# Layer 1 of a two-layer graph kernel: the mask added on four 64x64 tiles of TensorE, and six of 32 steps in which VectorE multiplies two heads

## The chip, the cores and the metric

The kernel runs on one core of a Trainium2 chip. The metric is the device time of one execution in microseconds (us); three runs are shown for the kernel before. A separate, profiled execution gives the trace from which all durations are taken.

## The reference

The input is `x` (4096 x 512) and a sparse matrix `adj` (4096 x 4096), nonzero on about 1.6% of its places and on the diagonal. Layer 0 is attention with an additive bias of 2 x `adj`; layer 1 is graph attention with eight heads of 64 features. The change touches layer 1 only:

```python
nX = (x @ W).reshape(n, NHEAD, OUT_DIM).transpose(1, 0, 2)
# nX is normalized over its 64 features
at1 = jnp.einsum('kno,ok->kn', nX, a1)[:, :, None]
at2 = jnp.einsum('kno,ok->kn', nX, a2)[:, :, None]
kg = jax.nn.leaky_relu(at1 + at2.transpose(0, 2, 1), negative_slope=LK_ALPHA)
kg = kg * graph[None, :, :]
mg = jnp.where(mask[None, :, :], kg, NEG_FILL)
attention = jax.nn.softmax(mg, axis=-1)
y = attention @ nX + nX
return jax.nn.elu(y)
```

So for each head and each pair of nodes there is a logit, the leaky ReLU of a sum of two numbers, multiplied by the edge's weight `graph`, masked where there is no edge, and put through an exponential before it weighs the features.

## The kernel before, in words

Layer 1 works on the transposed scores: sources lie on the 128 partitions, 512 target nodes on the free axis. A **step** is one block of 128 sources for 512 targets and four heads. There are 8 chunks of targets, 2 halves of the heads and 32 source blocks, so 512 steps. The 32 steps of one chunk and one half of the heads are called a **group** here (16 groups, 0 to 15). All engines follow an order that is written out by hand (`seq` keeps every instruction in program order on its engine). The loop over `n` runs, for each step: `values(n - 4)`, `exponent(n - 3)`, `leaky(n)`, `weigh(n)`, `z_sums(n + 1)`, `relu(n + 1)`.

- `z_sums` (TensorE, L955): for each of the four heads a matmul of six rows, `z2` against `z1` (L964), puts the sum of the two attention numbers into PSUM. The heads use different groups of 32 rows of the array. Then a matmul with the 128x128 identity (L969) adds the mask `nb`, which is a huge negative number where there is no edge. There are three PSUM tiles `d` of two banks each; a step needs two of them, one for heads 0 and 1 and one for heads 2 and 3.
- `relu` (ScalarE, L976) starts the leaky ReLU of heads 0 and 1 and writes the tile `t`, of which there are six.
- `leaky` (VectorE): two scalar_tensor_tensor instructions (L986) make the leaky ReLU of heads 3 and 2, a tensor_tensor (L991) multiplies by the edge weights `g`, and another (L992) completes heads 0 and 1.
- `weigh` (GpSimd, called POOL in profiles, L999) multiplies the heads that VectorE didn't by `g`.
- `exponent` (ScalarE, L1002) takes the exponential of all four heads in place.
- `values` (TensorE, L1015) multiplies `t` by the features `nX` in fp32, two heads side by side on 64 columns each, and accumulates over the group's 32 steps.

How the edge-weight multiply is shared is set by the set `light`: in an ordinary step VectorE multiplies one head and GpSimd three; in a step in `light` each multiplies two.

```python
light = {n + d for n in range(NB + 3, n_steps, NB) for d in (9, 10)}
```

That is steps 12 and 13 of every group but group 0 (30 steps), when GpSimd also has the ELU of the group before.

`finish` closes a group, spread over the first 14 steps of the next: ScalarE copies the sums out of PSUM (L1031), TensorE turns them to rows (L1037), VectorE divides (L1046, L1048) and adds the node's own features `own` into a tile `y` (L1049), ScalarE and GpSimd make the ELU (L1059 to L1077), and the rows are stored (L1081). `load_rows` (L947) loads `xi` and `own` for it from step 12 of a group on, on the queue of SP.

`load_adj` (L905) loads, on SP's queue and once per four steps, what the next four steps need: `z2`, the masks `nb` and the weights `g`. Each has two buffers. Group 0 also loads the features, and prepares the last 512 rows of layer 0's output (`make_ready`), some of it on GpSimd; the `own` products that `make_ready` spreads out reach into groups 1 to 4 (L360, L361).

Of the kernel before, what the change touches and what calls it, by code (L numbers as in the profile page):

```python
# [10 lines left out]
F32 = mybir.dt.float32  # L11
BF16 = mybir.dt.bfloat16
# [6 lines left out]
P = 128  # L19
N = 4096  # L20
D = 512
NH = 8
HD = 64
NB = N // P
SB = 4
# [10 lines left out]
GC = 512  # L36
# [42 lines left out]
def fast_path(  # L79
# [18 lines left out]
    nc = tc.nc  # L98
    seq = tc.keep_in_program_order
# [13 lines left out]
    const = ctx.enter_context(tc.tile_pool(name="const", bufs=1))  # L113
# [4 lines left out]
    ident_b = const.tile([P, P], BF16, name="ident_b")  # L118
# [24 lines left out]
    nT_d = dram.tile([NB, P, N], BF16, name="nT_d")  # L143
# [30 lines left out]
        return mv  # L174


    aa = [const.tile([P, NH, HD], F32, name=f"a{e}_sb") for e in (1, 2)]
    aln_sb = const.tile([P, HD], F32, name="aln_sb")
    bln2_sb = const.tile([P, HD], F32, name="bln2_sb")
    at_b = const.tile([P, 2, NH], F32, name="at_b")  # L180
# [279 lines left out]


    with tc.tile_pool(name="early", bufs=2) as early, tc.tile_pool(name="kv", bufs=1) as kv:
        v = kv.tile([P, NB, D], F32, name="v")
        TILES = [(ic, jt) for ic in range(NI) for jt in range(NB)]
        n_tiles = len(TILES)
# [66 lines left out]
        with tc.tile_pool(name="proj_c", bufs=1) as pc, tc.tile_pool(  # L532
            name="proj", bufs=2
# [125 lines left out]
            for k in range(KC):  # L659
                pa_ps = psum.tile([P, 512], F32, name="pa", tag="mm", bufs=4)  # L660
                for c in range(SB):
                    seq(nc.tensor.matmul(
                        pa_ps, turned["q"][:, c, ts(k, P)], turned["k"][:, c, :],
                        start=c == 0, stop=c == SB - 1,
# [6 lines left out]
            for sb in range(1, NS):  # L671
# [4 lines left out]
                if sb == 1:  # L676
                    seq(nc.sync.dma_start(
                        out=w1_sb.rearrange("p k h e -> p k (h e)"),
                        in_=w1.rearrange("(k p) o -> p k o", p=P),
# [16 lines left out]
        with tc.tile_pool(name="attn", bufs=2) as work, tc.tile_pool(  # L696
            name="attn_ps", bufs=2, space=PSUM
# [142 lines left out]
            for s in range(0, n_tiles, 2):  # L840
                ic, jt = TILES[s]
# [48 lines left out]
    with tc.tile_pool(name="ga_in", bufs=2) as inputs, tc.tile_pool(  # L890
# [4 lines left out]
        JB = 4  # L895
# [3 lines left out]
        inverses = gat.tile([P, NI, 2, 2, 2, 4], F32, name="inverses")  # L899
        loads, logits, zs, groups = {}, {}, {}, {}  # L900

        light = {n + d for n in range(NB + 3, n_steps, NB) for d in (9, 10)}
        later = {}

        def load_adj(q):  # L905
            ic, _, jt = STEPS[q * JB]
            z2 = inputs.tile([P, JB * P], BF16, name="z2", tag="z2", bufs=2)
            seq(nc.sync.dma_start(
                out=z2, in_=z2_d[:, STEPS[q * JB][1], jt * P : (jt + JB) * P]
            ))  # L910
            ng = inputs.tile([P, JB, GC], BF16, name="nb", tag="nb", bufs=2)
            seq(nc.sync.dma_start(
                out=ng, in_=nT_d[jt : jt + JB, :, ts(ic, GC)].rearrange("t p i -> p t i")
            ))
            g = adjs.tile([P, JB, GC], F32, name="g", tag="g", bufs=2)
            seq(nc.sync.dma_start(
                out=g, in_=gT_d[jt : jt + JB, :, ts(ic, GC)].rearrange("t p i -> p t i")
            ))
            loads[q] = (g, ng, z2)

        def cols(ic, hg):
            rows = slice(ic * GC, (ic + 1) * GC)
# [32 lines left out]
        def z_sums(n):  # L955

            ic, hg, jt = STEPS[n]
            _, ng, z2 = loads[n // JB]
            pair = [None, None]
            for hf in (1, 0):  # L960
                pair[hf] = psum.tile([P, 2, GC], F32, name="d", tag="d", bufs=3)
            for hh in (2, 3, 0, 1):
                rows = slice(32 * hh, 32 * hh + 6)
                seq(nc.tensor.matmul(  # L964
                    pair[hh // 2][:, hh % 2, :], z2[rows, ts(jt % JB, P)],
                    groups[ic, hg]["z1"][rows, :], start=True, stop=False,
                ))
            for hh in (2, 3, 0, 1):
                seq(nc.tensor.matmul(  # L969
                    pair[hh // 2][:, hh % 2, :], ident_b, ng[:, jt % JB, :], start=False, stop=True  # L970
                ))
            zs[n] = pair

        def relu(n):
# [45 lines left out]
        def finish(n, ic, hg):  # L1020

            grp = groups.pop((ic, hg))
            ob = work.tile([P, 2, GC], F32, name="ob", tag="ob", bufs=1)
            y = work.tile([P, 2, SB * 2, HD], F32, name="y", tag="y", bufs=1)

            def room():
                grp["e"] = work.tile([P, 2, SB * 2, HD], F32, name="e", tag="ob", bufs=1)

            def copies():
                for hf in range(2):  # L1030
                    seq(nc.scalar.copy(ob[:, hf, :], grp["acc"][hf]))  # L1031

            def to_rows(hf):
                pt = psum.tile([P, 2, GC], F32, name="pt1", tag="d", bufs=3)
                for b in range(SB):
                    col = (b % 2) * 2 * HB
                    seq(nc.tensor.matmul(  # L1037
                        pt[:, b // 2, col : col + 2 * HB], ob[:, hf, ts(b, P)],
                        back.rearrange("p e c -> p (e c)"), start=True, stop=True,
                    ))  # L1040
                grp["pt"] = pt[:, :, 0 : 4 * HB].rearrange("p k (q c) -> p k q c", c=HB)

            def divide(hf):
                v = grp.pop("pt")
                rinv = inverses[:, ic, hg, hf]
                seq(nc.vector.reciprocal(rinv, v[:, :, :, HD]))  # L1046
                v = v[:, :, :, 0:HD]
                seq(nc.vector.tensor_mul(v, v, rinv.unsqueeze(3).to_broadcast([P, 2, 4, HD])))  # L1048
                seq(nc.vector.tensor_add(  # L1049
                    y[:, hf].rearrange("p (k q) e -> p k q e", k=2), v,  # L1050
                    grp["own"][:, hf].rearrange("p b d -> p (b d)")
                    .rearrange("p (k q e) -> p k q e", k=2, e=HD),
                ))

            def flat(t):
                return t.rearrange("p f q e -> p (f q e)")

            def minus(hf):
                seq(nc.scalar.activation(grp["e"][:, hf], y[:, hf], AF.Relu, scale=-1.0))  # L1059

            def exps(hf):
                e = grp["e"][:, hf]
                seq(nc.scalar.activation(e, e, AF.Exp, scale=-1.0))

            def positive():
                seq(nc.scalar.activation(flat(y), flat(y), AF.Relu))

            def less_one():
                seq(nc.scalar.add(flat(grp["e"]), flat(grp["e"]), -1.0))

            def elu():
                e = flat(grp["e"])
                seq(nc.gpsimd.tensor_add(e, e, flat(y)))  # L1073

            def close():
                e = grp["e"]
                seq(nc.gpsimd.tensor_add(  # L1077
                    flat(e), flat(e), grp["xi"].rearrange("p f b d -> p (f b d)")
                ))
                for f, ap in enumerate(pair_rows(out, ic, hg)):  # L1080
                    nc.sync.dma_start(  # L1081
                        out=ap, in_=e[:, f].rearrange("p (b h) e -> p b (h e)", h=2)
                    )

            for d, place, f in (
                (0, "mid", copies),
                (1, "mid", lambda: to_rows(0)), (1, "end", lambda: divide(0)),
                (2, "mid", lambda: to_rows(1)), (2, "end", lambda: divide(1)),
                (4, "end", room), (4, "end", lambda: minus(0)), (5, "end", lambda: minus(1)),
                (6, "end", lambda: exps(0)), (6, "end", positive), (7, "end", lambda: exps(1)),  # L1090
                (8, "end", less_one),
                (9, "end", elu), (10, "end", close),
            ):
                later.setdefault((n + d, place), []).append(f)
# [34 lines left out]
        for n in range(n_steps + 15):  # L1129

            q = n // JB + 1
            if n == 1:
                store_rows(NI - 1, last_rows)
            if n % JB == (2 if q == NS - 1 else 0) and q < n_steps // JB:
                load_adj(q)
                if q < NS:
                    load_features(q)
            if n < n_steps and STEPS[n][2] == 12:
                load_rows(n)
            if n + 10 < n_steps and STEPS[n + 10][2] == 0:  # L1140
                open_group(n + 10, nc.sync)
            extra(n, "top")
            if 0 <= n - 4 < n_steps:
                values(n - 4)
                if n % JB == 3:
                    loads.pop((n - 4) // JB)
                if STEPS[n - 4][2] == NB - 1:
                    finish(n, *STEPS[n - 4][:2])
            if 0 <= n - 3 < n_steps:
                exponent(n - 3)  # L1150
            extra(n, "mid")
            for f in left.pop(n, []):
                f()
            if n % JB == 2 and n // JB < NS:
                ones_in(n // JB)
            if n < n_steps:
                leaky(n)
                weigh(n)
            if n + 1 < n_steps:
                z_sums(n + 1)  # L1160
                relu(n + 1)
            for f in left_late.pop(n, []):
                f()
            extra(n, "end")
# [425 lines left out]
```

## Time and profile before

| | |
|---|---|
| median of 3 runs | 3963.34 us (3960.78 to 3963.43) |
| the profiled execution | 3960.13 us, its span 3958.2 us |
| TensorE busy | 3786.1 us, 96% of the span |
| VectorE busy | 2889.7 us, 73% |
| GpSimd busy | 2569.7 us, 65% |
| ScalarE busy | 1796.8 us, 45% |
| layer 1 | about 2080 us to the end |
| DMA in layer 1 | about 45% busy, some 145 GB/s |
| L969, masks | 2048 matmuls, 385 ns each, 536.3 us busy |
| L999, GpSimd's multiplies | 512, mean 3410 ns |

A row of the profile's groups gives the line, the engine, the operation, output and inputs, the shapes and the number of instructions; then the busy time in us and the mean duration in ns; then the idle time of the engine just before them and who ended it. A row of a timeline gives the start in us, the duration, the engine and the group, merged when several alike follow each other (x4). The durations of matmuls overlap because they are pipelined; so do those of VectorE's instructions, by about 0.08 us, and the distance from start to start is then the better measure. The profile calls `z2` and `z1` just `z`, `u4` `u`, and so on, since numbers in names are left out.

### The profile page before, as it was taken

The numbers are of one execution on the slowest core, as the hardware profiler recorded it, in microseconds if no ns is written. First come the engines' busy times: TensorE is split into PE (matmuls) and PEld (weight loads), VectorE is DVE, ScalarE is ACT, GpSimd is POOL, SyncE is SP. The second block draws the span as 40 slices with busy tenths as digits, with TensorE's granted clock in tenths as the row PEclk, the third lists the DMA queues.
The fourth block names the chain that finished last, engine by engine and source line by source line (L and its number), as shares of the span: only waits on it lengthen the run. The fifth ranks groups of instructions, "written<-read, shape, count | busy, mean of one in ns | idle before, by whom it ended". The sixth has DMA issues, their size and how long they took to land. (4 is left out here: it accounts for less than half of the span.)

```text
span 3958.2 us, 44075 instructions
## 1 busy us (share of the span) xinstructions
PE 3786.1 (96%) x15370; PEld 1788.6 (45%) x15370; DVE 2889.7 (73%) x4331; ACT 1796.8 (45%) x1581; POOL 2569.7 (65%) x1305
## 2 busy tenths in 40 slices
PE   8989999999999999999998899999999999999997
PEld 4446666666666666666652222222222222222222
DVE  5435556565565656556557899999999999999996
ACT  1000111111111111111115788888888888888886
POOL 3432225243242525234257999999999999999998
PEclk9999999999999999999998999999999999999999
DMA  6466657667675766768557544444444444444442
GB/s 214 169 213 195 198 175 207 199 194 213 182 220 161 223 182 191 215 183 223 164 158 190 149 141 141 145 146 138 140 138 145 140 146 146 146 139 146 129 151 79
DMA packets 554407, 670.37 MB, mean 169 GB/s; under 512 B 79808, under 2 KB 397504, under 8 KB 534720
## 3 DMA queue, kind: packets, MB, share of 16 engines
q1 hardware_dynamic: 552112, 665.70, 56.5%
q8 instruction: 122, 2.00, 0.2%
q10 hardware_dynamic: 2064, 1.77, 0.2%
q14 instruction: 109, 0.89, 0.1%
HBM read 495.12 MB, written 172.23 MB: 169 GB/s over the span
## 5 line engine op out<-in xcount | busy, mean ns | idle before, releaser
L999 POOL TENSOR_TENSOR t<-t,g 128x1536 f32<-128x1536 f32 (+1 forms) x512 | 1722.8, 3410 | 34.3 <-DVE t L992 29.1
L1015 PE MATMUL acc<-t,nX 128*64 128x512 f32 x4096 | 994.5, 606 | 66.8 <-ACT t L1002 54.5
L751 POOL TENSOR_TENSOR total<-total,aT 128x512 f32<-128x512 f32 x248 | 340.3, 1372 | 1061.3 <-ACT aT L746 1051.1
L1002 ACT ACTIVATE t<-t 128x2048 f32<-128x2048 f32 x512 | 975.9, 1906 | 85.8 <-POOL t L999 84.6
L761 PE MATMUL acc<-v,aT 128*128 128x512 f32 x2048 | 961.9, 592 | 0.0
L746 ACT ACTIVATE aT<-aT 128x512 f32<-128x512 f32 x256 | 161.2, 630 | 1322.8 <-DVE aT L741 1314.8
L992 DVE TENSOR_TENSOR t<-t,d 128x1024 f32<-128x1024 f32 x512 | 619.9, 1211 | 12.3 <-ACT t L976 12.3
L976 ACT ACTIVATE t<-d 128x1024 f32<-128x1024 f32 x512 | 524.8, 1025 | 227.7 <-PE d L969 205.0
L969 PE MATMUL d<-nb,ident_b 128*128 128x512 bf16 x2048 | 536.3, 385 | 1.5 <-DMA nb<-nT_d 1.5
L1015 PEld LDWEIGHTS acc<-t,nX 128*64 128x64 f32 x4096 | 250.4, 136 | 595.3 <-issue 340.1
L761 PEld LDWEIGHTS acc<-v,aT 128*128 128x128 f32 x2048 | 389.7, 190 | 272.4 <-issue 244.9
L986 DVE SCALAR_TENSOR_TENSOR d<-u,at2m,d 128x512 f32<-128x512 f32 x542 | 407.0, 751 | 50.1 <-PE d L969 35.2
L741 DVE TENSOR_TENSOR aT<-aT,X 128x256 f32<-128x256 f32 x512 | 214.9, 420 | 280.5 <-PE X L733 277.3
L986 DVE SCALAR_TENSOR_TENSOR t<-u,at2m,d 128x512 f32<-128x512 f32 x482 | 360.0, 747 | 49.2 <-DVE d L986 0.9
L741 DVE TENSOR_TENSOR aT<-aT,Z 128x256 f32<-128x256 f32 x384 | 159.6, 416 | 292.3 <-PE Z L733 287.6
L991 DVE TENSOR_TENSOR t<-d,g 128x512 f32<-128x512 f32 (+1 forms) x512 | 366.0, 715 | 5.1 <-DMA g<-gT_d 1.8
L725 DVE SCALAR_TENSOR_TENSOR gs<-ng,aT 128x512 f32<-128x512 bf16 x256 | 285.8, 1117 | 10.1 <-DMA gT_d<-gs 1.4
L964 PE MATMUL d<-z,z 6*128 6x512 bf16 x2048 | 250.1, 385 | 35.2 <-DVE t L991 15.4
L964 PEld LDWEIGHTS <-z 6*128 6x128 bf16 x2048 | 76.4, 91 | 443.2 <-issue 439.1
L733 PE MATMUL Z<-qt,hS 128*128 128x256 f32 x1024 | 265.7, 382 | 9.0 <-DVE aT L741 8.3
L969 PEld LDWEIGHTS <-ident_b 128*128 128x128 bf16 x2048 | 159.2, 98 | 241.6 <-issue 121.9
L733 PE MATMUL X<-qt,hS 128*128 128x256 f32 x1024 | 263.8, 380 | 0.0
(170 smaller groups left out, 3124.9 us busy)
## 6 DMA issues: line engine op xcount, KB each, us to landing
g<-gT_d SPq DMA_DIRECT2D x128, 1024.0 KB, 5.5
ag<-in_adj_dram SPq DMA_DIRECT2D x256, 256.0 KB, 5.7
hT<-h_d SPq DMA_DIRECT2D x64, 1024.0 KB, 5.9
hS<-s_d SPq DMA_DIRECT2D x64, 1024.0 KB, 8.3
gT_d<-gs SPq DMA_DIRECT2D x256, 256.0 KB, 3.0
nb<-nT_d SPq DMA_DIRECT2D x128, 512.0 KB, 5.1
nT_d<-ng SPq DMA_DIRECT2D x256, 128.0 KB, 3.4
z<-z_d SPq DMA_DIRECT2D x143, 128.0 KB, 4.7
```

What stands on the lines that cost most here:

```text
L733: seq(nc.tensor.matmul(out, a, b, start=start and k == 0, stop=k == 1, skip_group_check=not start,))
L741: seq(nc.vector.tensor_add(p, p, part))
L751: seq(nc.gpsimd.tensor_add(totals[ic], totals[ic], p))
L761: seq(nc.tensor.matmul(sums[ic][b], probs[s][:, ts(b, P)], v[:, jt, :], start=jt == 0, stop=jt == NB - 1))
L969: seq(nc.tensor.matmul(pair[hh // 2][:, hh % 2, :], ident_b, ng[:, jt % JB, :], start=False, stop=True))
L976: seq(nc.scalar.activation(t[:, 0:2, :], zs[n][0], AF.Relu, scale=4.0))
L986: seq(nc.vector.scalar_tensor_tensor(pair[1][:, e, :] if e > 1 - mine else t[:, 2, :], u4[:, e, :], at2m[:, jt, h : h + 1], pair[1][:, e, ...
L991: seq(nc.vector.tensor_mul(t[:, HG - mine : HG, :], pair[1][:, 2 - mine : 2, :], g))
L992: seq(nc.vector.tensor_add(t[:, 0:2, :], t[:, 0:2, :], pair[0]))
L999: seq(nc.gpsimd.tensor_mul(t[:, 0:mine, :], t[:, 0:mine, :], g))
L1002: seq(nc.scalar.activation(logits[n], logits[n], AF.Exp))
L1015: seq(nc.tensor.matmul(grp["acc"][hf][ts(e, HD), :], nX[jt // SB][:, jt % SB, hg * HG + 2 * hf + e, :], t[:, 2 * hf + e, :], start=jt == 0 ...
```

## The change

The mask is no longer added by one 128x128 matmul for each head. Each half of 64 rows of the array serves one of two heads. For a head, its half adds the mask of partitions 0 to 63 to output partitions 0 to 63 on one 64x64 tile, and that of the other 64 partitions on the tile beside it. [...]a second copy of the masks, `nx`, is loaded with the two halves swapped. There are eight matmuls of 64x64x512 per step instead of four of 128x128x512. Further, `light` holds steps 1, 8, 12, 13, 19 and 25 of every group, group 0 included; `y` is written over `own`; `load_rows` comes at step 20; and the tiles `aa` move to a pool that ends with layer 0.

```diff
-    aa = [const.tile([P, NH, HD], F32, name=f"a{e}_sb") for e in (1, 2)]
+    aa = []
...
+        aa.extend(kv.tile([P, NH, HD], F32, name=f"a{e}_sb") for e in (1, 2))
...
-        light = {n + d for n in range(NB + 3, n_steps, NB) for d in (9, 10)}
+
+        light = {n for n in range(n_steps) if n % NB in (1, 8, 12, 13, 19, 25)}
...
+            nx = inputs.tile([P, JB, GC], BF16, name="nx", tag="nx", bufs=2)
+            for r in range(2):
+                seq(nc.sync.dma_start(
+                    out=nx[ts(r, HD)],
+                    in_=nT_d[jt : jt + JB, ts(1 - r, HD), ts(ic, GC)].rearrange("t p i -> p t i"),
+                ))
...
-            loads[q] = (g, ng, z2)
+            loads[q] = (g, (ng, nx), z2)
...
-            for hh in (2, 3, 0, 1):
-                seq(nc.tensor.matmul(
-                    pair[hh // 2][:, hh % 2, :], ident_b, ng[:, jt % JB, :], start=False, stop=True
-                ))
+
+            for first in (2, 0):
+                for r, c in ((0, 0), (1, 1), (0, 1), (1, 0)):
+                    hh, rows = first + r, ts(r, HD)
+                    seq(nc.tensor.matmul(
+                        pair[hh // 2][ts(c, HD), hh % 2, :], ident_b[rows, rows],
+                        masks[r != c][rows, jt % JB, :], start=False, stop=True,
+                    ))
...
-            y = work.tile([P, 2, SB * 2, HD], F32, name="y", tag="y", bufs=1)
+            y = grp["own"].rearrange("p f b (h e) -> p f (b h) e", e=HD)
...
-                seq(nc.vector.tensor_add(
-                    y[:, hf].rearrange("p (k q) e -> p k q e", k=2), v,
-                    grp["own"][:, hf].rearrange("p b d -> p (b d)")
-                    .rearrange("p (k q e) -> p k q e", k=2, e=HD),
-                ))
+                own = y[:, hf].rearrange("p (k q) e -> p k q e", k=2)
+                seq(nc.vector.tensor_add(own, v, own))
...
-            if n < n_steps and STEPS[n][2] == 12:
+            if n < n_steps and STEPS[n][2] == 20:
```

More of the change, by code (lines that the diff above doesn't have):

```diff
@@ L957, in z_sums @@
             ic, hg, jt = STEPS[n]
-            _, ng, z2 = loads[n // JB]
+            _, masks, z2 = loads[n // JB]
             pair = [None, None]
```

## The prediction

> **What bounds the kernel now.** I read the slices first, then the costliest groups, then the timelines of single engines in layer 1, which the change alone touches.
>
> ```profile
> PE   8989999999999999999998899999999999999997
> ...
> DVE  5435556565565656556557899999999999999996
> ...
> POOL 3432225243242525234257999999999999999998
> ...
> L999 POOL TENSOR_TENSOR t<-t,g 128x1536 f32<-128x1536 f32 (+1 forms) x512 | 1722.8, 3410 | 34.3 <-DVE t L992 29.1
> ...
> L992 DVE TENSOR_TENSOR t<-t,d 128x1024 f32<-128x1024 f32 x512 | 619.9, 1211 | 12.3 <-ACT t L976 12.3
> ...
> L969 PE MATMUL d<-nb,ident_b 128*128 128x512 bf16 x2048 | 536.3, 385 | 1.5 <-DMA nb<-nT_d 1.5
> ```
>
> From slice 22 on (layer 1) three engines show 9s, so busy shares can't name the limit. GpSimd (POOL) almost never idles: its 512 mask multiplies take 1722.8 us. Grouped by form between 2400 and 3900 us, 399 three-head multiplies keep it busy 1367.3 us, 3.427 each. Its timeline at a group's end:
>
> ```profile
> 3081.19 2.41 POOL L1073 TENSOR_TENSOR e<-e,y 128x1024 f32<-128x1024 f32 x1
> 3083.51 2.42 POOL L999 TENSOR_TENSOR t<-t,g 128x1024 f32<-128x1024 f32 x1
> 3085.85 2.42 POOL L1077 TENSOR_TENSOR e<-e,xi 128x1024 f32<-128x1024 f32 x1
> 3088.19 105.15 POOL L999 TENSOR_TENSOR t<-t,g 128x1536 f32<-128x1536 f32 x31
> ```
>
> A two-head multiply advances GpSimd 2.34 us (3083.51 to 3085.85), each finish operation about 2.33. So GpSimd needs per group of 32 steps 30 x 3.427 + 2 x 2.34 + 2 x 2.33 = 112.15 us (the row of 31 holds the second two-head multiply: 30 x 3.427 + 2.34 = 105.15). The starts of L992 in VectorE's timeline give the real length: 3031.08 to 3143.20, 112.1 us. **GpSimd sets the group's length.** But VectorE is right behind it:
>
> ```profile
> 3078.07 1.54 DVE L986 SCALAR_TENSOR_TENSOR d<-u,at2m,d 128x512 f32<-128x512 f32 x2
> 3080.06 1.22 DVE L991 TENSOR_TENSOR t<-d,g 128x1024 f32<-128x1024 f32 x1 [0.46 <-DVE d L986]
> 3081.20 1.21 DVE L992 TENSOR_TENSOR t<-t,d 128x1024 f32<-128x1024 f32 x1
> 3082.33 0.75 DVE L986 SCALAR_TENSOR_TENSOR d<-u,at2m,d 128x512 f32<-128x512 f32 x1
> 3083.18 0.75 DVE L986 SCALAR_TENSOR_TENSOR t<-u,at2m,d 128x512 f32<-128x512 f32 x1
> 3083.85 0.68 DVE L991 TENSOR_TENSOR t<-d,g 128x512 f32<-128x512 f32 x1
> 3084.45 1.21 DVE L992 TENSOR_TENSOR t<-t,d 128x1024 f32<-128x1024 f32 x1
> 3085.58 0.75 DVE L986 SCALAR_TENSOR_TENSOR d<-u,at2m,d 128x512 f32<-128x512 f32 x1
> ```
>
> The start-to-start distances 0.85 + 0.67 + 0.60 + 1.13 make 3.25 us, and this repeats step after step (3082.33 to 3124.53: 13 steps, 3.246 each) with no gap but 0.1 us behind the first L986. After every group end VectorE catches up at its own floor of 3.246 until the six `t` buffers are full; then it follows GpSimd at 3.43.
>
> ```profile
> 3084.50 0.48 PE L964 MATMUL d<-z,z 6*128 6x512 bf16 x4
> ...
> 3084.91 1.04 PE L969 MATMUL d<-nb,ident_b 128*128 128x512 bf16 x4
> ...
> 3085.88 1.94 PE L1015 MATMUL acc<-t,nX 128*64 128x512 f32 x8
> ```
>
> TensorE has the same 3.25: 0.41 from the z sums to the masks, 0.97 from masks to values, 1.87 to the next z sums. These start 0.05 after L992 (3084.50 against 3084.45), that is when L991 has freed the PSUM pair: VectorE releases TensorE, and TensorE has next to no slack.
>
> **What the skill says.** GPSIMD Engine Reference, section 3.1, puts GpSimd 1.96 times slower than VectorE on an fp32 tensor_tensor; here 2.38 against 1.21 us for 128x1024, so it agrees. TensorEngine Tiling (Array Packing), Key Properties: different tiles run weight loads and matmuls in parallel. The trace agrees for row tiles (four z sums within 0.48 us, one alone 0.385) and for column tiles (eight value matmuls in 1.94 us at a mean of 0.606); no run here shows 64x64 tiles. Its Gotcha 1 wants different row tiles in different PSUM banks; here they belong to different heads, each with its own bank.
>
> **The change part by part, against the profiled execution: span 3958.2, time 3960.1 us.**
>
> 1. *GpSimd.* Two-head steps go from 2 in each of 15 groups (30) to 6 in each of 16 (96). Each of the 66 spares GpSimd 3.427 - 2.34 = 1.09 us, 72 us in all. A group: 26 x 3.427 + 6 x 2.34 + 4.66 = 107.8.
>
> 2. *VectorE.* A two-head step took 3.91 us (3074.16 to 3078.07): 0.66 more than 3.246, because L991 doubles and both L986 write PSUM. 66 x 0.66 = 44 us more. The finish costs 1.575 twice (a step of 4.82 against 3.246). Busy floor of a group: 26 x 3.246 + 6 x 3.91 + 3.15 = **111.0 us**, above GpSimd's 107.8. Before, it was 108.35. VectorE becomes the bound, so most of GpSimd's 4.3 us a group can't be collected.
>
> 3. *Waits on top of that floor.* Group 1 before was already VectorE-bound (2240.53 to 2351.11: 110.6 us), so its waits can be read: 0.4 to 0.5 for the finish transposes (L1046 on PE L1037), and in the steps where ScalarE does the ELU 0.21 + 0.35 + 0.82 = 1.38 (L992 on ScalarE 0.27, L986 on PE 0.72). About 1.9 us. (A further 0.35 belongs to GpSimd's `own`, which only groups 1 to 4 have.)
>
> 4. *Masks.* Four passes of about 0.215 us become two, if four tiles run at once: 0.43 us less per step on TensorE. In ordinary steps it is hidden: z sums still wait for L991, and the STT starts behind L992 in any case (1.13 after L991's end, against 1.10 through TensorE today). It pays where TensorE or ScalarE is late: STT's masks are ready 0.2 earlier, ScalarE's `relu` and the values 0.43 earlier. I take the 1.9 of waits down to 0.9. Unknown: it could take them to 0 or leave all. Eight weight loads instead of four, even at the full 98 ns of today's row and exposed, would be 0.78, still below today's 0.85 of passes; a gain below the two passes is excluded by the 512 columns each must stream.
>
> So a group should take 111.0 + 0.9 = 111.9 us. From the L992 of step 32 (2240.53) to that of step 511 (3924.31) there are 15 groups less one step: 15 x 111.9 - 3.25 = 1675.3, against 1683.8: **-8.5**. Most of it is in groups 2 to 4, which GpSimd's `own` multiplies (2.56 us, L360 and L361) stretched to 114.6 (2351.11 to 2694.88); the groups of 112.1 give 0.2 each, group 1 loses 1.3.
>
> 5. *Group 0* (149.7 us) is a chain of TensorE, ScalarE and VectorE around the last rows' preparation. Masks earn 0.2 in some 20 exposed steps, six two-head steps cost up to 4: I take -2, between -6 and +3.
>
> 6. *Loads.* SP issues two more DMAs per four steps (about 0.36 us each, behind `nb`, ahead of `g`), 0.5 MB more on 1.6 MB. DMA is 45% busy, `g` waits for GpSimd anyway (942 us of SP's waits), which will be less behind: nothing, covered by the load being one block ahead; if that cover failed, L991 would wait for `g` every fourth step. At the very start it is exposed: z, `nb` and `g` took 2080.68 to 2090.21, 1.6 MB in 9.5 us; 0.5 MB more is up to 3. I take +2.5 (1 to 3).
>
> 7. *The end.* From the last L992 (3924.31) GpSimd still works off multiplies until 3934.39, 10.1 us, because it lags. A GpSimd that keeps up has 1.2 + 3.4 left: -5.4 (0 if it still lags).
>
> 8. *`own` written in place, `load_rows` at step 20 instead of 12, `aa` in an earlier pool.* The four row loads move past no later load that is due: L1046 needs them 12 steps on. SP no longer stands up to 8.9 us for GpSimd's `close` (116 us in 13 waits, L952 on L1077); nothing waited behind that in the trace: 0. The in-place add keeps its duration (0.69).
>
> Sum: -8.5 - 2 + 2.5 - 5.4 = -13.4, so 3946.7 on the profiled execution. The median of the runs (3963.3) lies 3.2 above that execution; I predict **3950 us**.
>
> **Rivals.**
> - *A, the forecast*: VectorE is the bound, about 3950. With waits gone: 15 x 0.9 = 13.5 less, group 0 at -6: 3932. With all waits left: 15 more and group 0 at +3: 3970. Chance 0.72, three quarters of it below 3955.
> - *B, VectorE has room*: GpSimd stays the bound and its 72 us come out, 3890. For it: GpSimd idles nowhere now. Against: VectorE's unbroken rows. 0.05.
> - *C, slower*: the four tiles run only two at a time, so masks still take four passes, TensorE is no earlier, and the waits around the group's end stay, with drains of the new shape: groups of 113.2 to 113.5 instead of 112.1, start +2.5, group 0 +3, end -5 to 0: 3970 to 3985. For it: TensorE has no slack today. It decides once the waits exceed 1.7 us a group. 0.17.
> - *D, tiles don't overlap at all*: eight passes, 0.85 us more each step, 512 x 0.85 = 435 us: 4390. Against: both kinds of tile overlap in the trace. 0.06.
>
> **Numbers.** About 0.2% (8 us) is what a measurement here can tell from no change. Faster: 0.75 of A and B, 0.59. Within: 0.16 of A and a third of C, 0.22. Slower: the rest (0.02 of A, two thirds of C, D), 0.19. The range runs from A's best (3931) to C's lower part (3972). A's own range is 3932 to 3970.
>
> **What would show it.** Right: GpSimd below 99% busy in layer 1 and waiting on L992; L992 starts 111 to 113 us apart between groups; L969 in two bunches of four; two-head steps of 3.9 us. Wrong: ordinary steps away from 3.25 (the floor was not VectorE's own), groups near 108 (B), a period above 4 us (D), or L991 waiting for `g`.

## The result, and the profile after

The kernel after takes **3955.62 us** (median of 20; 3952.11 to 3959.64), the kernel before, measured beside it, 3962.72 us (3960.28 to 3967.42): a ratio of 0.9982, 95% interval 0.9975 to 0.9988. The gain of 7.1 us is clear of zero by this interval, but it is less than the 8 us that the prediction took as the least it could tell from no change. The profiled execution took 3958.11 us, its span is 3956.2.

The slices and the costliest groups of the profile after, as they were shown of before:

```profile
PE   8989999999999999999997799999999999999997
...
DVE  5435556565565656556556799999999999999997
...
POOL 3432225243342525234156899999999999999998
...
L1012 POOL TENSOR_TENSOR t<-t,g 128x1536 f32<-128x1536 f32 (+1 forms) x512 | 1655.3, 3293 | 98.3 <-DVE t L1005 66.4
...
L1005 DVE TENSOR_TENSOR t<-t,d 128x1024 f32<-128x1024 f32 x512 | 619.9, 1211 | 6.6 <-ACT t L989 6.6
...
L981 PE MATMUL d<-nb,ident_b 64*64 64x512 bf16 x2048 | 319.9, 391 | 2.7 <-DMA nb<-nT_d 2.7
L981 PE MATMUL d<-nx,ident_b 64*64 64x512 bf16 x2048 | 320.3, 391 | 1.1 <-DMA nx<-nT_d 1.1
```

L1012 was L999, L1005 was L992, L981 was L969. GpSimd's idle time ahead of its multiplies has grown from 34.3 to 98.3 us, and VectorE's L1005 ends most of it: GpSimd now waits for VectorE. VectorE's own wait at L1005 has halved, to 6.6. The stretch 2400 to 3800 us before and after (busy time of PE, of PEld, which is TensorE's weight loads, of DVE, ACT and POOL, then TensorE's granted clock, DMA share and GB/s):

```profile
2400.00:3800.00 1400.00, 1333.98 (x6570) 399.59 (x6568) 1320.51 (x1667) 1192.21 (x893) 1399.84 (x429) 1.00 0.45 143
```
```profile
2400.00:3800.00 1400.00, 1275.23 (x8212) 350.69 (x8212) 1345.76 (x1676) 1186.46 (x901) 1358.00 (x432) 1.00 0.63 181
```

GpSimd is busy for 1358.0 of 1400 us instead of 1399.84, VectorE for 1345.76 instead of 1320.51.

The timeline of the kernel after, one two-head step and the start of the next, mid-group (start in us, duration, engine):

```profile
3035.78 1.54 DVE L999 SCALAR_TENSOR_TENSOR d<-u,at2m,d 128x512 f32<-128x512 f32 x2
...
3037.43 1.23 DVE L1004 TENSOR_TENSOR t<-d,g 128x1024 f32<-128x1024 f32 x1
...
3038.58 1.21 DVE L1005 TENSOR_TENSOR t<-t,d 128x1024 f32<-128x1024 f32 x1
...
3038.72 0.39 PE L973 MATMUL d<-z,z 6*128 6x512 bf16 x2 [0.78 <-DVE t L1004]
...
3039.04 0.40 PE L981 MATMUL d<-nb,ident_b 64*64 64x512 bf16 x2
3039.04 0.40 PE L981 MATMUL d<-nx,ident_b 64*64 64x512 bf16 x2
3039.28 0.38 PE L981 MATMUL d<-nb,ident_b 64*64 64x512 bf16 x2
3039.28 0.38 PE L981 MATMUL d<-nx,ident_b 64*64 64x512 bf16 x2
...
3039.70 0.75 DVE L999 SCALAR_TENSOR_TENSOR d<-u,at2m,d 128x512 f32<-128x512 f32 x1
```

The eight masks go in two bunches of four, 0.24 us apart, and are done in 0.62 us where four large ones took 1.04. Within a bunch all four tiles overlap. The step from L999 to L999 lasts 3.92 us (3035.78 to 3039.70); VectorE has no gap over 0.1 us, and TensorE waits 0.78 for its L1004.

The start of layer 1 (timeline of VectorE, of TensorE and of SP's queue):

```profile
2089.07 0.64 PE L981 MATMUL d<-nb,ident_b 64*64 64x512 bf16 x2 [2.74 <-DMA nb<-nT_d]
```
```profile
2097.77 0.69 DVE L1004 TENSOR_TENSOR t<-d,g 128x512 f32<-128x512 f32 x1 [4.18 <-DMA g<-gT_d]
```
```profile
2091.40 6.94 SPq L920 DMA_DIRECT2D nx<-nT_d  x2
2098.62 0.37 SPq L925 DMA_DIRECT2D g<-gT_d  x1
```

The first step waits 2.74 us for `nb` and then 4.18 us for `g`, which stands in the queue behind `nx`. The row of 6.94 us holds both `nx` loads of the next block: the second is issued only at its end, when `g` has landed.

### The profile page after: what moved, and what is told of

Same layout as the page of the kernel before. It is cut to its first block, busy times and chain, and to the rows that moved or that the text cites. A ratio compares the mean times of both kernels' runs of the same rounds, so it can differ in the third digit from the quotient of the medians.

```text
span 3956.2 us, 48595 instructions
## 1 busy us (share of the span) xinstructions
PE 3699.6 (94%) x17418; PEld 1720.8 (43%) x17418; DVE 2915.4 (74%) x4331; ACT 1779.3 (45%) x1581; POOL 2501.9 (63%) x1305
## 5 line engine op out<-in xcount | busy, mean ns | idle before, releaser
L1012 POOL TENSOR_TENSOR t<-t,g 128x1536 f32<-128x1536 f32 (+1 forms) x512 | 1655.3, 3293 | 98.3 <-DVE t L1005 66.4
L1005 DVE TENSOR_TENSOR t<-t,d 128x1024 f32<-128x1024 f32 x512 | 619.9, 1211 | 6.6 <-ACT t L989 6.6
L973 PE MATMUL d<-z,z 6*128 6x512 bf16 x2048 | 382.7, 387 | 140.5 <-DVE t L1004 76.5
L999 DVE SCALAR_TENSOR_TENSOR d<-u,at2m,d 128x512 f32<-128x512 f32 x608 | 456.2, 750 | 33.3 <-PE d L981 29.8
L1004 DVE TENSOR_TENSOR t<-d,g 128x512 f32<-128x512 f32 (+1 forms) x512 | 402.0, 785 | 16.6 <-DMA g<-gT_d 7.0
L973 PEld LDWEIGHTS <-z 6*128 6x128 bf16 x2048 | 94.4, 91 | 663.2 <-issue 400.9
L999 DVE SCALAR_TENSOR_TENSOR t<-u,at2m,d 128x512 f32<-128x512 f32 x416 | 310.8, 747 | 43.2 <-DVE d L999 1.4
L981 PE MATMUL d<-nb,ident_b 64*64 64x512 bf16 x2048 | 319.9, 391 | 2.7 <-DMA nb<-nT_d 2.7
L981 PE MATMUL d<-nx,ident_b 64*64 64x512 bf16 x2048 | 320.3, 391 | 1.1 <-DMA nx<-nT_d 1.1
```

The costliest lines, as they stand in the source:

```text
L973: seq(nc.tensor.matmul(pair[hh // 2][:, hh % 2, :], z2[rows, ts(jt % JB, P)], groups[ic, hg]["z1"][rows, :], start=True, stop=False,))
L981: seq(nc.tensor.matmul(pair[hh // 2][ts(c, HD), hh % 2, :], ident_b[rows, rows], masks[r != c][rows, jt % JB, :], start=False, stop=True,))
L999: seq(nc.vector.scalar_tensor_tensor(pair[1][:, e, :] if e > 1 - mine else t[:, 2, :], u4[:, e, :], at2m[:, jt, h : h + 1], pair[1][:, e, ...
L1004: seq(nc.vector.tensor_mul(t[:, HG - mine : HG, :], pair[1][:, 2 - mine : 2, :], g))
L1005: seq(nc.vector.tensor_add(t[:, 0:2, :], t[:, 0:2, :], pair[0]))
L1012: seq(nc.gpsimd.tensor_mul(t[:, 0:mine, :], t[:, 0:mine, :], g))
```

## The experiments

All times are medians, and every ratio is to runs of the kernel before that were measured beside them. A **group length** is the distance between the L1005 (or its successor) of the first steps of two groups that follow each other, read from one trace of each kernel.

### Each part alone

`e1_tiles_only`: the kernel after, with the two-head steps of before.

```diff
-        light = {n for n in range(n_steps) if n % NB in (1, 8, 12, 13, 19, 25)}
+        light = {n + d for n in range(NB + 3, n_steps, NB) for d in (9, 10)}
```

> The changed kernel with the two-head steps of the kernel before (12 and 13, none in group 0); the tiles, the second copy of the masks and all else stay. Theory (GpSimd sets the group's length, TensorE's relief alone buys nothing): groups 5 to 14 at 112.1 us, groups 2 to 4 at 114.6, GpSimd 99 to 100% busy, and the cost of the extra loads at the start and in group 0 on top: 3965 to 3972 us, slower than the kernel before by 3 to 9. Rival (TensorE held the steps back, the tiles alone bring the gain): groups near 111.8 and 3950 to 3957.

Measured: 3968.58 us, ratio 1.0012 (1.0005 to 1.0018). Groups 2 to 4 take 114.6 to 114.7 us, the later ones about 112.1, as before: GpSimd is busy for 1399.84 of 1400 us (2400 to 3800). The tiles alone bring nothing, because they speed up an engine that waits. The 4.6 us more are about what the start costs: from layer 0's last division to the first L1005 17.6 us instead of 13.7.

`e2_six_steps_only`: the kernel before, with the six two-head steps.

```diff
-        light = {n + d for n in range(NB + 3, n_steps, NB) for d in (9, 10)}
+        light = {n for n in range(n_steps) if n % NB in (1, 8, 12, 13, 19, 25)}
```

> The kernel before with two-head steps 1, 8, 12, 13, 19 and 25 of every group, masks still on 128x128. Theory (VectorE's busy floor of 111.0 plus the waits that the faster masks remove): groups at 112.7 to 113.2, waits in step 4 of 0.4 to 0.5 and in step 12 of 0.8 still there, no loss at the start: 3960 to 3968 us, no gain over the kernel before. Rival (the tiles do nothing at all for the period, the six steps alone are the gain): groups of 111.8 and, without the extra loads, 3945 to 3950.

Measured: 3966.24 us, ratio 1.0004 (0.9995 to 1.0012). Groups of 112.62 us nearly throughout, so the 114.6 of groups 2 to 4 is gone and the rest is 0.5 longer. With six steps the tiles are worth 112.62 - 111.77 = 0.85 us a group: from one step's last VectorE instruction to the next one's, 0.37 from step 4 to 5, 0.33 from 10 to 11 and 0.19 from 11 to 12. (The smaller changes, `own` in place, the later `load_rows` and the moved `aa`, are in this difference too; no run parts them from the tiles.) **Neither part gains alone.** The steps make VectorE the bound, and only then are the waits that the tiles shorten on the path.

### Group 0 and the start

`e3_tiles_from_group1`: the second copy is loaded, and the tiles are used, from group 1 on.

```diff
+            nx = None
+            if q * JB >= NB:
+                nx = inputs.tile([P, JB, GC], BF16, name="nx", tag="nx", bufs=2)
-            for r in range(2):
+            for r in range(2 if q * JB >= NB else 0):
...
+            if n < NB:
+                for hh in (2, 3, 0, 1):
+                    seq(nc.tensor.matmul(
+                        pair[hh // 2][:, hh % 2, :], ident_b, masks[0][:, jt % JB, :],
+                        start=False, stop=True,
+                    ))
-            for first in (2, 0):
+            for first in (2, 0) if n >= NB else ():
```

> The changed kernel, but group 0 adds its masks as before, and the second copy is loaded from group 1 on. Theory (the second copy's loads hold up g and the features at the start and in group 0): the first L992 follows the end of layer 0 as early as before (about 13 us after the first division), group 0 at 147 to 150 us, the rest unchanged at 111.8 per group: 3945 to 3949 us. Rival (group 0 is longer because of the six two-head steps in it, or by chance from run to run): 3953 to 3957.

Measured: 3953.25 us, ratio 0.9975 (0.9966 to 0.9984). That is the rival's time; 3945 to 3949 was expected. From layer 0's last division (L804) to the first step's last VectorE instruction (L1013 here) it takes 15.3 us instead of 19.2 (before: 13.7), but group 0 stays at 153.32 us: the start was `nx`, the length of group 0 mostly something else.

### Which engine sets the period

`e5_less_vector`: L1005 adds only the term of head 0; that of head 1 is left out, so this run is for the time alone.

```diff
-            seq(nc.vector.tensor_add(t[:, 0:2, :], t[:, 0:2, :], pair[0]))
+            seq(nc.vector.tensor_add(t[:, 0:1, :], t[:, 0:1, :], pair[0][:, 0:1, :]))
```

> The changed kernel, but the last VectorE instruction of a step (L1005) adds only head 0 and leaves out head 1's second term: 512 elements less, about 0.53 us less per step on VectorE and nothing else. Theory (VectorE alone sets the group): VectorE's floor falls to 94, GpSimd's 107.8 takes over: ordinary steps at 3.3 to 3.45, groups at 107.8 to 108.3, about 3895 to 3905 us. Rival (TensorE, ScalarE or the PSUM hand-over hold the 3.25): groups stay above 110.5.

Measured: 3904.3 us (one run). The stretch 3000 to 3100 us, columns as above:

```profile
3000.00:3100.00 100.00, 91.84 (x604) 25.49 (x600) 86.51 (x125) 87.97 (x68) 100.00 (x32) 1.00 0.63 180
```

With less to do VectorE falls to 86.5% and GpSimd to 0 idle. Groups 8 to 14 take 107.2 to 108.4 us, mostly 107.7, which is the 107.8 that the prediction's first step gave as GpSimd's own need (the earlier ones scatter more, 106.7 to 111.1). So in the kernel after **VectorE is the bound**, and GpSimd has 4 us less to do.

`e4_four_steps`: the kernel after with four two-head steps, a share between the two.

```diff
-        light = {n for n in range(n_steps) if n % NB in (1, 8, 12, 13, 19, 25)}
+        light = {n for n in range(n_steps) if n % NB in (12, 13, 19, 25)}
```

> The changed kernel with four two-head steps in a group (12, 13, 19, 25) instead of six. Theory (VectorE is the bound with six; with four it needs 109.7 busy + 0.7 of waits and GpSimd 110.0): groups 5 to 14 at 110.2 to 110.8, groups 1 to 4, which hold GpSimd's own multiplies, 111.8 to 112.7: 3941 to 3948 us. Rival (GpSimd is still the bound with six): 4 x 0.5 x 1.09 more per group, near 114, and 3985.

Measured: 3941.16 us, ratio 0.9948 (0.9935 to 0.9962). Groups 5 to 14 take 110.42 us (two of them 110.7 and 110.8), so a two-head step costs (111.77 - 110.42) / 2 = 0.67 us. Groups 1 to 4, which all hold GpSimd's `own` multiplies, take 110.77, 111.12, 114.66 and 111.26: in group 3 step 19 alone waits 2.7 us.

`e8_tile_order`: the kernel after, the tiles of one row half right behind each other.

```diff
-                for r, c in ((0, 0), (1, 1), (0, 1), (1, 0)):
+                for r, c in ((0, 0), (0, 1), (1, 0), (1, 1)):
```

> The changed kernel with the four tiles of two heads in the order (0,0), (0,1), (1,0), (1,1), so that the tiles of one row group follow each other. Theory (four tiles overlap whatever their order): the eight mask matmuls again in two bunches within 0.65 us, groups at 111.8, 3950 to 3960 us. Rival (tiles that share rows queue up behind each other): three or four passes, masks 0.85 to 1.05 us, waits around the group's end back, groups at 112.6.

Measured: 3954.22 us (one run), groups of 111.67 us (three of 112.0 to 112.9), the masks done within 0.63 us. Between these two orders there is no difference to see.

`e6_combined`: from the last four: no tiles and no two-head steps in group 0 (the edit of `e3` and this), six in groups 1 to 4, four from group 5 on.

```diff
+        light = {
+            n for n in range(NB, n_steps)
+            if n % NB in ((12, 13, 19, 25) if n >= 5 * NB else (1, 8, 12, 13, 19, 25))
+        }
```

> Tiles from group 1 on; no two-head step in group 0, six in groups 1 to 4 and four (12, 13, 19, 25) in groups 5 to 15. Theory: groups 5 to 14 at 110.4, groups 1 to 4 at 111.8, group 0 back at 149 to 151 (its lengthening came from the two-head steps, not from the second copy), start 13.5 to 15.5 us after the first division: 3933 to 3939 us, faster than both. Rival (group 0 is longer by chance): group 0 at 153 and 3938 to 3942.

Measured: **3934.79 us**, ratio 0.9928 (0.9915 to 0.9942), faster than both kernels. Groups of 111.75 and then 110.43 us. Group 0 takes 150.9 us; whether it is shorter because of the two-head steps, as expected, or by scatter, one trace can't tell. What four two-head steps would give without the tiles was not run. An estimate from the 0.85 us above is 110.43 + 0.85 = 111.3 us a group, so the tiles should pay there too.

### The wait that is left, and what stands behind it

In `e6_combined` it still takes 4.53 us from step 11 to step 12, 0.62 more than a two-head step needs. The trace shows VectorE waiting for TensorE's masks there; I took the cause to be ScalarE, which in the steps before has ELU work between its own parts of the chain. `e7_spread_elu` spreads this over two more steps; the last group's closing add and its store fall outside the loop and are left out.

```diff
-                (6, "end", lambda: exps(0)), (6, "end", positive), (7, "end", lambda: exps(1)),
-                (8, "end", less_one),
-                (9, "end", elu), (10, "end", close),
+                (6, "end", lambda: exps(0)), (7, "end", lambda: exps(1)), (8, "end", positive),
+                (10, "end", less_one),
+                (11, "end", elu), (12, "end", close),
```

> The combined version with ScalarE's ELU spread out: the exponentials in steps 9 and 10, the positive part in step 11 instead of 9, the subtraction in 13 instead of 11, GpSimd's two additions in 14 and 15. Theory (the 0.62 us that step 12 still waits come from ScalarE being late after two operations in step 9): this wait goes down to 0 to 0.3, groups 5 to 14 at 109.8 to 110.2, 3927 to 3936 us. Rival (ScalarE is late in whichever steps it has the four operations): groups stay at 110.4.

Measured: 4019.18 us, ratio 1.0142 (1.0126 to 1.0157): a loss. The wait in step 12 is gone (3.90), so it was the ELU work, but from step 19 to step 20 it now takes 7.8 to 11.4 us. `e9_spread_one_step` spreads by one step (in the numbers of this diff: `less_one` 9, `elu` 10, `close` 11) and moves the two-head steps along (13, 14, 20, 26):

> The combined version with ScalarE's ELU spread by one step only: the exponentials in steps 9 and 10, the positive part in 11, the subtraction in 12, GpSimd's two additions in 13 and 14, and the two-head steps there moved along (13, 14, 20, 26, with 1 and 8 in groups 1 to 4). Theory (step 12's last wait of 0.62 us is ScalarE being late after two operations in one step; what made the wider spread slow was the store of the rows, which stood in SP's queue ahead of the next masks): the wait is gone, the store is out before the next loads are due, groups 5 to 14 at 109.7 to 110.0: 3924 to 3931 us. Rival (any later close holds up the loads): stalls on nb in step 20 or 21 and 3950 or more.

Measured: 3963.91 us, ratio 1.0001 (0.9992 to 1.0009): a miss. Steps 12 and 13 have no wait left, yet from step 19 to step 20, now a two-head step, it takes 5 to 8 us instead of 3.9. SP's queue, from the lists of waits of `e6_combined` and of `e9_spread_one_step`:

```profile
SPq L966 <- POOL e L1094: 63.0, 14, 5.0
```
```profile
SPq L966 <- POOL e L1094: 107.2, 14, 7.8
SPq L1102 <- POOL e L1098: 30.6, 14, 3.4
```

In these kernels the lines are shifted once more: the masks are L992, VectorE's last instruction of a step L1016, GpSimd's multiply L1023. L966 loads `own`, whose buffer is free once GpSimd's ELU add (L1094) has read it; L1102 stores the rows and waits for the closing add (L1098). Both now come later, and SP's loads of masks stand behind them (`e9_spread_one_step`):

```profile
3092.56 0.92 SPq L966 DMA_DIRECT2D own<-own_d  x2
...
3097.23 0.93 SPq L1102 DMA_DIRECT2D out_dram<-e  x2
3098.26 0.55 SPq L913 DMA_DIRECT2D z<-z_d  x1
3098.91 1.01 SPq L917 DMA_DIRECT2D nb<-nT_d  x1
3100.01 1.24 SPq L925 DMA_DIRECT2D nx<-nT_d  x2
```

My theory was the store. `e10_store_later` issues it behind the loads of step 20:

```diff
-                (10, "end", elu), (11, "end", close),
+                (10, "end", elu), (11, "end", close), (13, "mid", store),
...
-        for n in range(n_steps + 15):
+        for n in range(n_steps + 17):
```

> The one-step spread, but the row store is issued two steps after the step of GpSimd's closing add, behind the loads of the next group's step 16 in SP's queue. Theory (the 2 to 5 us stall at step 20 of the one-step spread came from z, nb and nx standing in SP's queue behind the store, which waits for GpSimd's closing add): the stall is gone, groups 5 to 14 take 109.7 to 110.0 us and groups 1 to 4 about 111.1, 3922 to 3931 us, faster than the combined version (3934.8). Rival (the stall comes from the loads that are bunched at that place, wherever the store stands): still over 3 us lost at step 20 of each group, 3945 us or more.

Measured: 3976.36 us, ratio 1.0031 (1.0023 to 1.0039). **The theory fell**: step 20 has no stall any more, but step 24 has one, with 5.7 to 8.9 us from step 23 to 24 in groups 5 to 14. `own` still waits 107.2 us at the head of the queue, and then rows and blocks go out together. The stretches of `e10_store_later` around such a stall (busy time of PE, TensorE's clock, DMA share, GB/s):

```profile
3105.00:3115.00 10.00, 9.12 (x60) 1.00 0.82 249
3115.00:3120.00 5.00, 4.77 (x36) 1.00 1.03 204
3120.00:3125.00 5.00, 2.98 (x17) 0.88 1.08 275
3125.00:3130.00 5.00, 5.00 (x17) 0.50 0.91 167
3130.00:3135.00 5.00, 5.00 (x30) 0.60 0.78 213
3135.00:3140.00 5.00, 4.41 (x34) 1.00 0.08 23
```

The transfer engines are full from 3115 to 3125 and TensorE runs dry. Then its clock is at half: 0.12, 0.50 and 0.40 of three stretches of 5 us were withheld, 5.1 us in all, which at half clock is 10.2 us. TensorE in that stretch:

```profile
3123.38 0.37 PE L992 MATMUL d<-nx,ident_b 64*64 64x512 bf16 x1 [1.00 <-DMA nx<-nT_d]
3124.65 0.58 PE L992 MATMUL d<-nx,ident_b 64*64 64x512 bf16 x1 [0.90 <-DMA nx<-nT_d]
...
3125.59 3.68 PE L1039 MATMUL acc<-t,nX 128*64 128x512 f32 x8
```

The same eight value matmuls take 3.68 us here and 1.94 at full clock. The Trainium skill's page "TensorE: Matmul & The Clock Gate", Part 1, puts the idle clock at half and names an idle window of about 3.4 us as what brings it. The trace agrees on the half. It does not show such an idle window: TensorE was busy for 2.98 of the 5 us, and its two waits for `nx` were 1.00 and 0.90 us.

This stall, in group 8, has the longest half clock of its run and costs the most; it is not the rule. In the seven other groups from 5 to 12 the half clock lasted 3.4 us each. In groups 13 and 14 the clock stayed full, although in group 14 TensorE was busy for only 2.78 of 5 us (3805 to 3810), with a wait of 2.62 us; these two groups still took 2.5 and 3.8 us more than the 109.80 of a group without stalls (group 8: 6.4 more). So waiting costs some us by itself, and the half clock comes on top in some stalls. What decides it stays open.

`e11_rows_in_order` also takes `own` off the head of the queue: row loads and store keep the order in which the program issues them, behind a block's loads.

```diff
-                    nc.sync.dma_start(out=t[:, f], in_=ap)
+                    seq(nc.sync.dma_start(out=t[:, f], in_=ap))
...
-                    nc.sync.dma_start(
-                        out=ap, in_=e[:, f].rearrange("p (b h) e -> p b (h e)", h=2)
-                    )
+                    seq(nc.sync.dma_start(
+                        out=ap, in_=e[:, f].rearrange("p (b h) e -> p b (h e)", h=2)
+                    ))
```

> The version before (ELU one step later, store behind the loads of step 20), with the row loads xi and own also held in order: behind the loads of step 24, instead of own standing ahead of those of step 20. Theory (own waits for GpSimd's ELU at the head of SP's queue, 107 us in 14 waits against 63 in the combined version, holds the loads of masks up, and then everything goes out in one bunch in which nx takes 12 us and more to land): no step over 5 us in groups 5 to 14, groups of 109.7 to 110.2, 3922 to 3931 us, faster than the combined version (3934.8). Rival (the bytes of the rows themselves fill the transfer engines around step 20 wherever they stand, and the masks come late): still a step of 5 to 9 us in each group, 3950 us or more.

Measured: 3972.34 us, ratio 1.0022 (1.0016 to 1.0029). SP no longer waits for GpSimd's ELU at all, and the stall is still there, now at step 28 (up to 9.1 us), right behind `xi`, `own`, `z1` and `u`, which now go out together: 1.6 MB of them ahead of a block of 2.1 MB. The rival was right: the bytes matter, wherever they stand. But a bunch alone is not enough. In `e6_combined` rows and blocks also go out together, the transfer engines are as full for 20 us (1.10 and 1.02 of their time), and nothing stalls:

```profile
3080.00:3090.00 10.00, 9.40 (x60) 2.45 (x60) 9.65 (x13) 8.70 (x7) 10.00 (x4) 1.00 1.10 264
3090.00:3100.00 10.00, 9.30 (x60) 2.46 (x60) 9.69 (x13) 8.08 (x7) 10.00 (x5) 1.00 1.02 253
```

There `own` goes out about 3.3 us earlier in its group than in `e9_spread_one_step`, which suggests that the cover was nearly used up already. Group 15, behind which no such loads come, has no stall and would make a group of 109.8 us (106.54 to its last L1016, and 3.25).

`e12_rows_spread` therefore deals them out, one kind to a block:

```diff
             if n < n_steps and STEPS[n][2] == 20:
-                load_rows(n)
-            if n + 10 < n_steps and STEPS[n + 10][2] == 0:
-                open_group(n + 10, nc.sync)
+                load_rows(n, ("own", own_d))
+            if n < n_steps and STEPS[n][2] == 24:
+                load_rows(n, ("xi", x1_d))
+            if n + 24 < n_steps and STEPS[n + 24][2] == 0:
+                open_group(n + 24, nc.sync)
```

> The version before, with the rows' transfers dealt out: z1 and u behind the loads of step 12, the store behind those of step 20, own behind those of step 24, xi behind those of step 28; no more than 0.6 MB beside any block of 2.1 MB. Theory (several row transfers next to one block are what makes that block's nx late): no step of a group over 5 us, groups 5 to 14 at 109.8 as group 15 of the version before, which has no such loads, 3922 to 3931 us, faster than the combined version (3934.8). Rival (any row transfer beside a block makes nx late now that the chain is tighter): stalls at two or more places of a group, of 1 us and more each, 3940 us or more.

Measured: **3922.39 us** (3921.42 to 3924.12), ratio 0.9895 (0.9879 to 0.9912), the fastest of all. Groups 5 to 14 take 109.80 us (two of them 110.2), groups 1 to 4 111.13. The stretch 2400 to 3800 us, columns as above:

```profile
2400.00:3800.00 1400.00, 1295.48 (x8350) 358.83 (x8349) 1353.30 (x1705) 1201.87 (x913) 1398.08 (x438) 1.00 0.65 183
```

DMA moves as much as in `e10_store_later` or `e11_rows_in_order` (2700 to 3800 us: 177 GB/s in both, 183 here), just evenly, and the waits for `nx` and `g` are gone from its list of waits. GpSimd is busy for 1398 of 1400 us and all of VectorE's waits in 2400 to 3900 us come to 0.9. By the prediction's figures GpSimd needs 28 x 3.427 + 4 x 2.34 + 4.66 = 110.0 us a group with four two-head steps and VectorE 28 x 3.246 + 4 x 3.91 + 3.15 = 109.7: their bills meet, and with this share of the work neither has anything left to give.

**Not all of this gain comes from the groups.** Of the 13.8 us between the profiled spans of `e6_combined` and of this kernel (3933.0 and 3919.2), 9.4 are in groups 1 to 15 and 5.8 in the start. The start had a cause that I had overlooked. In the kernel before, half of group 0's `xi` stands in SP's queue ahead of layer 1's first loads and waits 22.2 us there for VectorE, which scales layer 0's last rows (L808):

```profile
SPq L952 <- DVE x L808: 22.2, 1, 22.2
```
```profile
2080.27 0.36 SPq L952 DMA_DIRECT2D xi<-x_d  x1
2080.68 0.50 SPq L908 DMA_DIRECT2D z<-z_d  x1
```

The kernel after and every run but the last two have this wait too (22.1 to 22.5 us). In `e11_rows_in_order` the row loads keep the program's order, so the first `z`, `nb` and `g` go out some 12 us earlier, and the first step's last VectorE instruction comes 8.3 us after layer 0's last division, instead of 13.7 before. So in `e11_rows_in_order` the stalls cost more than its total shows.

## Why the prediction was right, and where it was not

The direction and the mechanism held: rival A. 3950 was predicted and 3955.6 measured, so about half of the gain of 13 us came. On the profiled executions -13.4 was summed and only -2.0 came, but some 5 us of this difference is the choice of executions: the one of before lies 2.6 us below its median, the one of after 2.5 above. A part of that can be seen ahead of the change: layer 0's last division came at 2079.15 instead of 2077.11 us, and over all runs that point scatters from 2076.9 to 2082.6. From there on it is -4.0 against -13.4, and the shortfall is in steps 5, 6 and 7.

- **Steps 1 to 4, the groups: right.** L1005 of step 32 to that of step 511: 2251.5 to 3926.3, 1674.8 us, against 1675.3 predicted and 1683.8 before. Nearly every group takes 111.77 us (predicted 111.9), groups 2 to 4 too, so most of the gain is there, as stated. A two-head step costs 3.91, an ordinary one 3.25. The waits, 1.9 before, came down to 0.73: 0.11 ahead of step 5 and 0.62 ahead of step 12. The 0.9 was about half of 1.9, chosen without a reason for the half, so that the sum fits so well is partly luck. GpSimd's 107.8 was seen bare in `e5_less_vector`. One reading was wrong: the further 0.35 us of group 1 doesn't belong to `own`, for a wait of that size also comes in groups 6 and 7 of the kernel after, where GpSimd has no `own`. Its cause is open.
- **Tiles.** The Trainium skill's page "TensorEngine Tiling (Array Packing)", Key Properties, says that different tiles work in parallel. No run showed it for 64x64 then; now the trace agrees, four at once, so rivals C and D fall with their first premise.
- **Step 5, group 0: missed, the cause open.** -2 (-6 to +3) predicted, +3.45 measured (153.16 against 149.71), from one trace of each kernel. Its first 22 steps did much as said, somewhat smaller: 105.10 us before, 102.73 with the tiles alone (`e1_tiles_only`), 104.64 with both. The term that was missed is the stretch of steps 22 to 26, where the last rows' numbers go through DRAM on the same queue: 25.12 us before, 29.03 after, with a wait of 2.80 for `g`. With `nx` in group 0 it took 27.6 to 29.0 (`e1`, `e4`, `e8`, after), without it 25.1 to 26.5 in seven (before, `e3`, `e6`, `e7`, `e9`, `e10`, `e12`). But two others without `nx` (`e2`, `e11`) show 28.7 and 28.9, so `nx` is not its only cause. In all the long ones TensorE's clock is at half for at least 10.2 us from step 24 on, before for 6.8 us from step 25; but `e12` has the 10.2 too and took 25.9. Which transfer is late there stays open. Some of the 3.45 may be scatter: four kernels whose group 0 is built alike (`e6`, `e7`, `e9`, `e10`) take 149.9 to 151.9, and `e8`, which differs from the kernel after in the order of the tiles alone, 151.4.
- **Step 6, the start: undersized.** +2.5 (1 to 3) predicted, 19.2 - 13.7 = +5.5 measured. Over all runs in which `xi` stands at the head of the queue the start takes 17.4 to 19.7 us with `nx` in group 0 and 12.8 to 15.8 without, so `nx` costs some 4 us, more than the range in any case. The estimate took the bytes at the rate of the start. What it left out is in the timeline above: `nx` delays `nb` and `g` one after the other, and the first step waits for both. In the steady state the transfers were indeed free, as said; but the cover is thin, as `e9` to `e11` showed, with DMA at 0.63 instead of 0.45 of its time.
- **Step 7, the end: -4.0 instead of -5.4.** 33.93 us from the last L992 to the end of the span before, 29.95 from the last L1005 after. GpSimd had 6.5 us left behind the last L1005, not 4.6: it still lagged a little.
- **Step 8: 0**, as far as can be seen: no run has these three changes alone, but the groups of 112.1 us stayed at that in `e1_tiles_only`, which has them. In `e9_spread_one_step` something late was queued behind, and it cost.

## What to carry to other kernels

Where two engines are nearly tied, write down what each needs per period, with its waits, and choose the share at which the bills meet: six two-head steps overshot, four were 1.35 us a group better. A faster engine off the path pays nothing until the work is moved so that its waits are on the path. Loads that an in-order queue hides are hidden by their spacing, not by their average: the same bytes cost about 4 us a group in one bunch (`e11_rows_in_order`) and nothing when dealt out over the blocks. And look at what stands at the head of such a queue where a new stage begins: one load that was not needed yet held up the first loads of layer 1, and with it out of the way the first step was done 5.4 us earlier than in the kernel before (8.3 instead of 13.7 us).

## What the hardware showed that I had not expected

- TensorE's granted clock can fall to 0.50 without any wait over 1.00 us: in the stall shown, for 10.2 us, in which the eight value matmuls take 3.68 instead of 1.94 us. Of the nine other stalls in groups 5 to 14 seven had 3.4 us of half clock and two none, one of these in spite of a wait of 2.62 us. So a late transfer can cost more than the wait shows, but it need not.
- The two orders in which the four 64x64 tiles were issued make no difference, even with two of the same rows behind each other (111.67 against 111.77 us a group).
